# A spiking recommender on one core: filler transposes of the identity behind every transpose of the first stage

## The chip, the cores and the metric

The kernel runs on one core of one Trainium2 chip. The metric is the time of one execution on the device in microseconds (us), the median of three runs. Engines are named as in the profile: PE (matmuls and transposes; PEld its weight loads), DVE (vector), ACT (scalar), POOL (which issues the gathers) and SP (which issues plain DMAs).

## The reference, cut to what matters

The inputs are 1024 sequences of 50 item numbers, their lengths, and a table of 100001 rows of 128 floats. For every step t the row of the item is gathered and added to a running sum; the sum is divided by min(t, length), normalised over the batch, and fed into a leaky integrate-and-fire neuron. The mean of the spikes is multiplied by the whole table.

```python
e = emb[seq]                                  # 1024 x 50 x 128, row 0 counts as zero
prefix = jnp.cumsum(e, axis=1)
uF = prefix / denom[:, :, None]               # denom = min(t, length)
mean, var = uF.mean(axis=0), uF.var(axis=0)
y = (uF - mean) * lax.rsqrt(var + BN_EPS) * gamma + beta
def step(v, x):
    v = v + (x - v) / TAU
    spike = atan_spike(v - V_TH)              # 1 where v >= V_TH
    return v - spike * V_TH, spike
_, spikes = lax.scan(step, v0, x_seq)         # over the 50 steps
scores = spikes.mean(axis=0) @ emb.T          # 1024 x 100001
```

## The kernel before, in words

The program is written out in the order in which each engine works; there is no scheduler (`manual_schedule`), and each engine runs its own instructions in order.

**First stage** (lines 171 to 444): the 50 steps of the neuron, with the batch along the free dimension (1024 columns) and the 128 features on partitions. In step t:

- POOL has issued eight indirect DMAs (`gather`, line 204), each 128 rows of the table, into one of two tiles `e` (`gp`, line 177, two buffers). The gather of step t + 2 is issued after the transposes of step t and goes into the tile that they have read.
- PE transposes the eight blocks of 128x128 into `pre` (line 327), two PSUM banks `pre[0]` and `pre[1]`, adding to what is there: `pre` is the running sum. Four transposes make a half of the batch (`h`).
- DVE scales each half to `uF` (line 338) and takes statistics (339, 345).
- PE adds a correction for item 0 to each half for the next step (`correct`, lines 279 to 288, two matmuls of 512 columns). It must wait until DVE has read the half.
- ACT and DVE normalise and step the neuron: r, q, a (349 to 375), count (300), v (379, 382), d (293).

In steps 42 and 44 (`T - 8`, `T - 6`, lines 395 to 408) PE also prepares one piece of 1024 table rows: eight transposes into `pt` (line 136), which takes the PSUM buffer of an older v, followed by a copy on ACT (152) and a subtraction on DVE (153) that split the values in two parts, hi and lo. The first piece also has a small memset on DVE (133).

`warm` (line 305) is a tile of two PSUM banks that the second stage uses first as `po_0_0` (418). `keep_busy(tile, times)` (307 to 309) transposes a tile into it over and over; nobody reads the result. Before the change it is called in the last step behind three transposes, four times each (`KQ // 2`, with `KQ` = 8), and once after the loop, 16 times (414).

**Second stage** (446 to the end): for each block of columns of the output, and each of the eight blocks of 128 batch rows, PE multiplies the counts by hi and lo (line 160), ACT and DVE take turns in scaling the result out of PSUM (511, 513), and SP stores it (169). 409.6 MB are written.

Of the kernel before, what the change touches and what calls it, by code (L numbers as in the profile page):

```python
# [20 lines left out]
P = 128  # L21
# [3 lines left out]
KQ = HALF // P  # L25
BANK = 512
# [13 lines left out]
def rec_kernel(  # L40
# [34 lines left out]
    ident = const.tile([P, P], F32, tag="ident", name="ident")  # L75
# [96 lines left out]
    with ExitStack() as ph:  # L172
# [134 lines left out]
        def keep_busy(tile, times):  # L307
            for k in range(times):
                nc.tensor.transpose(warm[:, k % KQ * P : (k % KQ + 1) * P], tile, ident)
# [6 lines left out]
        for t in range(T):  # L316
            last = t == T - 1
# [7 lines left out]
            for h, cs in enumerate(halves):  # L325
                for k in range(0, BANK, P):
                    nc.tensor.matmul(  # L327
                        pre[h][:, k : k + P],
                        lhsT=e[:, h * BANK + k : h * BANK + k + P],
                        rhs=ident,  # L330
                        start=False,
                        stop=last,
                        is_transpose=True,
                        skip_group_check=True,
                    )
                    if last and h and k + P < BANK:
                        keep_busy(ident, KQ // 2)
                nc.vector.scalar_tensor_tensor(uF[:, cs], rlen[:, cs], 1.0 / (t + 1), pre[h], ALU.max, ALU.mult)  # L338
                nc.vector.bn_stats(bs[:, h, :], uF[:, cs])  # L339
# [123 lines left out]
    for c, W in enumerate(WIDTHS):  # L463
# [34 lines left out]
        for n in range(NB):  # L498
# [26 lines left out]
            if n in (1, 4) and c >= MIDDLE and to_fetch < parts:  # L525
                g, k = divmod(to_fetch - SHIFT, GROUP)
# [26 lines left out]
```

## Time and profile before

| what | before |
|---|---|
| median of 3 runs | 1643.39 us (1637.56 to 1649.35) |
| the profiled execution's own time | 1576.4 us |
| its span, first to last instruction | 1574.6 us |
| PE busy | 1128.4 us, 72% of the span |
| DVE busy | 949.3 us, 60% |
| ACT busy | 673.4 us, 43% |
| POOL busy | 380.9 us, 24% |
| bytes written to HBM | 409.60 MB |

The page's second part cuts the span into 40 slices of 39.4 us; each digit is the share of the slice in which the engine was busy, in tenths. Its fifth part groups instructions: line, engine, operation, what is written and read, count, then busy time in us and the mean of one in ns, then how long the engine stood idle just before them and what ended that. In a timeline a line is: start in us, duration in us, engine, line, operation, count (xN for N merged ones), and in brackets the idle time before it and what ended it. A busy time of a group of overlapping matmuls is less than count times mean. The page's clock digits are those of recorded clock events; where none had been recorded yet, they show full clock.

### The profile page before, as it was taken

The page shows a single profiled execution, that of the slowest core. Times are in us where ns is not written, and L with a number is a line of the kernel's source. Part 1 is how long each engine was busy: PE and PEld are TensorE (multiplying, and loading weights), DVE is VectorE, ACT ScalarE, POOL GpSimd, SP SyncE. Part 2 cuts the span into 40 slices and gives each one's busy share as a digit, 9 for nine tenths or more (in the row PEclk, how much of TensorE's full clock was granted, in tenths as well). Part 3 has the DMA queues.
Part 4 walks back from the last instruction along what each step waited for, and adds up shares of the span by engine and source line. Part 5 has one row for each costly group of instructions (what it writes and reads, how often), then busy time and mean ns, then how long its engine had stood idle before and what let it go on. Part 6 is the DMA issues. An engine that isn't in the chain of part 4 may idle for free.

```text
span 1574.6 us, 12255 instructions
## 1 busy us (share of the span) xinstructions
PE 1128.4 (72%) x4464; PEld 799.5 (51%) x4464; DVE 949.3 (60%) x1127; ACT 673.4 (43%) x697; POOL 380.9 (24%) x406
## 2 busy tenths in 40 slices
PE   4544444444445998899888878888878878888884
PEld 2211111111122766677766666666666666666663
DVE  5777777777777655666555555555555545555552
ACT  2333333333333545555444444444444444444442
POOL 7777777777776000000000000000000000000000
PEclk9999999999975999999999999898999999999998
DMA  9711111111121899999999999999999999999998
GB/s 347 264 52 54 52 54 52 53 53 54 52 79 47 337 414 414 423 413 402 428 427 429 427 426 421 421 409 429 421 428 424 402 428 429 414 423 417 426 405 354
DMA packets 51313, 488.12 MB, mean 310 GB/s; under 512 B 10079, under 2 KB 10336, under 8 KB 30004
## 3 DMA queue, kind: packets, MB, share of 16 engines
q1 hardware_dynamic: 30752, 430.86, 65.1%
q0 software_dynamic: 12800, 26.24, 5.7%
q10 hardware_dynamic: 7700, 30.23, 4.7%
q8 instruction: 35, 0.57, 0.1%
q14 instruction: 26, 0.21, 0.0%
HBM read 77.69 MB, written 409.60 MB: 309 GB/s over the span
## 4 chain that ended last, share of the span: by engine, by line
DMA 48%; POOL 18%; PE 15%; issue 8%; DVE 5%; ACT 4%; ACTq 0%; SPq 0%; POOLq 0%; DVEq 0%
DMA scores<-o 42%; POOL e L207 18%; PE po L160 14%; DMA e<-in_L_rec_emb_table,idx 6%; DVE o L511 3%; ACT o L513 3%; DVE pairs L153 1%; ACT pairs L152 0%; PE pt L136 0%; ACT hi L152 0%; DVE lo L153 0%; PE pre L327 0%; DMA idx<-in_r_seq 0%; DVE bs L339 0%; DVE uF L338 0%
## 5 line engine op out<-in xcount | busy, mean ns | idle before, releaser
L511 DVE TENSOR_SCALAR o<-po 128x1024 f32<-128x1024 f32 (+1 forms) x391 | 467.3, 1214 | 329.5 <-DMA scores<-o 187.4
L513 ACT ACTIVATE o<-po 128x1024 f32<-128x1024 f32 x391 | 392.0, 1025 | 506.0 <-DMA scores<-o 362.7
L207 POOL DMA_INDIRECT e<-in_L_rec_emb_table,idx x400 | 380.2, 951 | 123.9 <-issue 112.5
L327 PE MATMUL pre<-ident,e 128*128 128x128 f32 x400 | 179.9, 463 | 227.3 <-DMA e<-in_L_rec_emb_table,idx 227.0
L160 PE MATMUL po<-pairs,countB 128*128 128x512 f32 (+1 forms) x1120 | 292.8, 408 | 57.8 <-ACT o L513 57.8
L160 PE MATMUL po<-pairs,countC 128*128 128x512 f32 (+1 forms) x840 | 240.1, 433 | 59.4 <-ACT o L513 53.4
L160 PEld LDWEIGHTS po<-pairs,countB 128*128 128x128 f32 x1120 | 211.8, 194 | 119.2 <-ACT o L513 76.7
L327 PEld LDWEIGHTS pre<-ident,e 128*128 128x128 f32 x400 | 73.4, 184 | 337.1 <-DMA e<-in_L_rec_emb_table,idx 336.4
L160 PEld LDWEIGHTS po<-pairs,countC 128*128 128x128 f32 x840 | 168.1, 208 | 112.1 <-ACT o L513 65.5
L153 DVE TENSOR_TENSOR pairs<-pt,pairs 128x1024 fp32r<-128x1024 f32 x70 | 85.2, 1218 | 94.9 <-ACT pairs L152 94.8
L338 DVE SCALAR_TENSOR_TENSOR uF<-rlen,pre 128x512 f32<-128x512 f32 x100 | 68.3, 683 | 109.6 <-PE pre L327 109.6
L136 PE MATMUL pt<-ident,rows 128*128 128x128 f32 (+1 forms) x768 | 104.4, 281 | 9.9 <-issue 4.9
L349 ACT ACTIVATE r<-mv,eps 128x1 f32<-128x1 f32 x50 | 14.7, 295 | 223.4 <-DVE mv L345 223.4
L136 PEld LDWEIGHTS pt<-ident,rows 128*128 128x128 f32 (+1 forms) x768 | 94.1, 147 | 27.1 <-issue 10.9
L160 PE MATMUL po<-hi,countB 128*128 128x512 f32 x208 | 85.6, 411 | 15.1 <-ACT o L513 13.5
L281 PE MATMUL pre<-zT,ls 128*128 128x512 f32 x100 | 77.5, 777 | 23.2 <-DVE uF L338 19.3
L152 ACT CAST pairs<-pt 128x1024 fp32r<-128x1024 f32 x70 | 70.1, 1014 | 41.2 <-PE pt L136 41.2
L160 PE MATMUL po<-lo,countB 128*128 128x512 f32 x208 | 83.4, 401 | 0.0
L293 ACT ACTIVATE d<-v,less 128x1024 bf16<-128x1024 f32 x49 | 54.6, 1114 | 64.8 <-DVE v L382 62.3
L160 PE MATMUL po<-hi,countC 128*128 128x512 f32 x156 | 66.7, 427 | 14.1 <-ACT o L513 12.6
L379 ACT ACTIVATE v<-uF,hgb,a 128x1024 f32<-128x1024 f32 x49 | 59.2, 1208 | 30.6 <-DVE a L375 30.5
L339 DVE BATCH_NORM_STATS2 bs<-uF 128x6 f32<-128x512 f32 x100 | 69.4, 694 | 3.5
(87 smaller groups left out, 851.8 us busy)
## 6 DMA issues: line engine op xcount, KB each, us to landing
scores<-o SPq DMA_DIRECT2D x96, 3072.0 KB, 19.8
scores<-o SPq DMA_DIRECT2D x32, 1536.0 KB, 8.9
scores<-o SPq DMA_DIRECT2D x30, 1024.0 KB, 7.9
rows<-in_L_rec_emb_table ACTq DMA_DIRECT2D x19, 1536.0 KB, 29.3
scores<-o SPq DMA_DIRECT2D x8, 2896.5 KB, 17.2
rows<-in_L_rec_emb_table SPq DMA_DIRECT2D x5, 3072.0 KB, 34.9
e<-in_L_rec_emb_table,idx POOLq DMA_INDIRECT x400, 2.5
rows<-in_L_rec_emb_table SPq DMA_DIRECT2D x2, 1024.0 KB
```

The costliest lines, as they stand in the source:

```text
L136: nc.tensor.transpose(pt[:, k0 : k0 + pw], r[:pw, k0 : k0 + D], ident[:pw, :pw])
L152: nc.scalar.copy(vh, vp)
L153: nc.vector.tensor_tensor(vl, vp, vh.bitcast(F32), ALU.subtract)
L160: nc.tensor.matmul(po[:, :kw], lhsT=counts[n], rhs=part[:, k0 : k0 + kw], start=j == 0, stop=j == 1,)
L207: nc.gpsimd.indirect_dma_start(out=es[t][:, n * P : (n + 1) * P], out_offset=None, in_=table, in_offset=bass.IndirectOffsetOnAxis(ap=idx[: ...
L281: nc.tensor.matmul(pre[h], lhsT=l, rhs=zT[:, h * BANK : (h + 1) * BANK], start=t == 0, stop=False, skip_group_check=True,)
L327: nc.tensor.matmul(pre[h][:, k : k + P], lhsT=e[:, h * BANK + k : h * BANK + k + P], rhs=ident, start=False, stop=last, is_transpose=True, ...
L338: nc.vector.scalar_tensor_tensor(uF[:, cs], rlen[:, cs], 1.0 / (t + 1), pre[h], ALU.max, ALU.mult)
L339: nc.vector.bn_stats(bs[:, h, :], uF[:, cs])
L379: nc.scalar.activation(vt, uF[:, cs], AF.Identity, bias=hgb[:, 1:2], scale=a)
L511: nc.vector.tensor_scalar_mul(o[:, h0 : h0 + hw], po[:, :hw], 1.0 / T)
L513: nc.scalar.mul(o[:, h0 : h0 + hw], po[:, :hw], 1.0 / T)
```

## The change

Behind each of the eight transposes of line 327, in every step but the last, PE now transposes the identity nine times (`KQ + 1`) into `warm`. In the last step the fillers stay as they were.

```diff
@@ -333,7 +333,9 @@
                         is_transpose=True,
                         skip_group_check=True,
                     )
-                    if last and h and k + P < BANK:
+                    if not last:
+                        keep_busy(ident, KQ + 1)
+                    elif h and k + P < BANK:
                         keep_busy(ident, KQ // 2)
                 nc.vector.scalar_tensor_tensor(uF[:, cs], rlen[:, cs], 1.0 / (t + 1), pre[h], ALU.max, ALU.mult)
                 nc.vector.bn_stats(bs[:, h, :], uF[:, cs])
```

## The prediction

> **What bounds the kernel now.** I read the page's parts 1, 2 and 5 first, then the timeline of one step (around 265 us), of the end of the first stage (500 to 522 us) and of the two steps that also prepare table rows (434 to 474 us), and last the table of windows for the granted clock.
>
> ```profile
> span 1574.6 us, 12255 instructions
> ...
> PE   4544444444445998899888878888878878888884
> ...
> POOL 7777777777776000000000000000000000000000
> ...
> L207 POOL DMA_INDIRECT e<-in_L_rec_emb_table,idx x400 | 380.2, 951 | 123.9 <-issue 112.5
> L327 PE MATMUL pre<-ident,e 128*128 128x128 f32 x400 | 179.9, 463 | 227.3 <-DMA e<-in_L_rec_emb_table,idx 227.0
> ```
>
> The first stage is the 12.9 slices in which POOL works, 0 to about 511 us. PE is less than half busy there and waits for gathers. POOL never waits for anything but its own 0.30 us issue: a gather each 0.95 + 0.30 = 1.25 us. The timeline shows the beat:
>
> ```profile
> 264.20 0.94 POOL L207 DMA_INDIRECT e<-in_L_rec_emb_table,idx  x1 [0.30 <-issue]
> 265.45 0.95 POOL L207 DMA_INDIRECT e<-in_L_rec_emb_table,idx  x1 [0.30 <-issue]
> 265.48 0.18 PEld L327 LDWEIGHTS pre<-ident,e 128*128 128x128 f32 x1 [1.07 <-DMA e<-in_L_rec_emb_table,idx]
> 266.67 0.18 PEld L327 LDWEIGHTS pre<-ident,e 128*128 128x128 f32 x1 [1.01 <-DMA e<-in_L_rec_emb_table,idx]
> 267.19 0.69 DVE L338 SCALAR_TENSOR_TENSOR uF<-rlen,pre 128x512 f32<-128x512 f32 x1 [2.47 <-PE pre L327]
> 267.93 0.79 PE L281 MATMUL pre<-zT,ls 128*128 128x512 f32 x1 [0.35 <-DVE uF L338]
> ```
>
> Eight gathers make a step of 10.0 us. The transpose is 1.0 us of waiting and little work. So the stage is POOL's 400 x 1.25 = 500 us; nothing that makes PE faster there can shorten it, and PE matters only if its own step passes 10.0 us or if it falls so far behind that something waits.
>
> What a filler costs, and at which clock, stands at the stage's end and in the second stage:
>
> ```profile
> 504.49 0.48 PE L327 MATMUL pre<-ident,e 128*128 128x128 f32 x1
> 504.75 1.06 PE L309 MATMUL warm<-ident 128*128 128x128 f32 x4
> 507.28 2.61 PE L309 MATMUL warm<-ident,near 128*128 128x128 f32 x16
> ...
> 741.32 1.03 PE L136 MATMUL pt<-ident,rows 128*128 128x128 f32 x8
> ```
>
> Four cold fillers: (1.06 - 0.421 of one) / 3 = 0.213 us apart. Eight warm transposes of the same shape: (1.03 - 0.271) / 7 = 0.109 us apart. In the 16, durations fall from 421 to 273 ns and the window 508 to 509 us has a clock of 0.65 between 0.50 and 1.00. The stage before is cold, whatever its row of clock digits says: the same transposes take 470 ns and more at 265 us.
>
> [...] a burst of nothing but 16 transposes at 443.5 to 447.2 us left the next matmul at 0.50 us where that line takes 0.77 to 0.80, and the fillers of 503.6 to 508.7 us, with PE idle some 0.15 us in each 1.25, lifted the clock as well. [...]
>
> **The change part by part.** It adds 49 x 8 x 9 = 3528 pairs of weight load and transpose, no wait, no DMA, and removes nothing.
>
> 1. *Steady steps.* Warm PE work: 8 x 10 x 0.109 = 8.72 us, plus the two corrections of line 281 at about 0.226 us each (pitch of the warm 128x512 matmuls of line 160: 12 in 2.88 us, one 0.39): 0.45. Sum 9.17 us, under 10.0. It hides behind the gathers, with 0.83 us to spare per step. Per gather PE is busy some 1.1 of 1.25 us, as busy as the fillers that lifted the clock, so it should stay warm. DVE's uF needs only the transposes before the last nine, and the correction's wait for uF (1.26 us now) is filled by those nine. Cost 0. Without the warm clock the step would be 80 x 0.213 + 2 x 0.43 = 17.9 us.
>
> 2. *First step.* Its eight gathers have landed by 16.4 us and PE is cold. Fillers run cold to about 20.6 us [...]: 20 of the 80. The other 60 take 6.6 us: done 27.2, the last real one at 26.2 to 26.5. Step 2's gather overwrites the same e buffer (two buffers, lines 177 and 205) and was issued at 25.15. POOL loses 1.4 us, for good. [...]
>
> 3. *Steps 42 and 44* (lines 395 to 408). Here PE, in order, waits for DVE before it can prepare table rows, while gathers pile up:
>
> ```profile
> 443.30 0.17 DVE L133 MEMSET rows<- 1x128 f32 x1
> 443.56 1.94 PE L136 MATMUL pt<-ident,rows 128*128 128x128 f32 x8 [4.87 <-issue]
> 445.30 1.91 PE L327 MATMUL pre<-ident,e 128*128 128x128 f32 x8
> 448.46 0.50 PE L281 MATMUL pre<-zT,ls 128*128 128x512 f32 x1 [1.25 <-DVE uF L338]
> ...
> 462.02 1.94 PE L136 MATMUL pt<-ident,rows 128*128 128x128 f32 x8 [3.31 <-DVE count L300]
> ```
>
> Before, the backlog of eight went through in 1.9 us. Now it carries 72 fillers, and the 5 us of idling have made PE cold. Walking it through: preparing ends 445.1; cold to 447.3, one group of ten; seven groups x 1.09 = 7.6, to 454.9 (last real transpose 453.9, before 446.8); corrections to 455.4. Step 44: 8.7 us, to 464.1, last real 463.1 against 456.7: 6.4 us late. Its count on DVE ends 4.8 us after uF starts, so PE waits again to 468.3, prepares cold to 470.0, and is cold to about 473: step 45's last real one at 479.2. Each later step takes 8.7 + 0.5 = 9.2 us: 488.4 (step 46), 497.6 (47), 506.8 (48), where before has 497.0. The lag of 9.8 us shrinks by only 0.8 a step and has four steps. Step 46 ending at 488.4 also holds the gather of step 48 (485.8 before) 2.9 us; that lies inside the lag.
>
> 4. *End.* From step 48's last transpose on, DVE and ACT run a chain without slack (497.55 to 511.1 us: uF, statistics, count twice, negv, near, the last uF). It moves by 9.8 less 0.2 for warm latency = 9.6 us. The last step's fillers are unchanged and 20 transposes take 2.2 us, hidden behind that chain.
>
> 5. *Second stage.* Unchanged work, already at full clock at 511 us. Stores start at 513 us and share DMA with nothing before, and later blocks wait on them, so a late start passes through. Gain from a warm PE at its opening: nothing left to gain.
>
> Sum: 1.4 + 9.6 = 11.0 us. On the profiled execution 1576.4 + 11.0 = 1587.4; its span is 1574.6. The median of the runs, 1643.39, lies 67 us above the profiled one, and nothing in the profile says where; I add the difference to the median: 1654.4. Bounds of it: no re-cooling at both waits makes the lag 5.5 us[...]: +5 to +15.
>
> **Rivals.**
> - *A, hidden.* The two waits of DVE shrink or the lag is absorbed: 0 to +5, so 1643 to 1649. For it: DVE is busy only 7.2 us a step (71.9 of 100 us in the table of windows). Against: PE gains back only 0.8 us a step.
> - *B, uF waits for the ninth filler* if the semaphore comes behind them. Then the correction ends 1.2 us after the fillers, the step is 8.7 + 1.2 = 9.9 us, and no lag is ever made up: the first step's 7.5 us add to the later ones, about +20 to +25: 1666. Against: each instruction here is followed by its own waiter.
> - *C, PE does not stay warm.* It decides once the mean pitch passes (10.0 - 0.5) / 80 = 0.119 us. All cold: (17.9 - 10.0) x 48 = +380, 2020 us. Half the time: +170, 1815. [...] against: both bursts above.
> - *D, faster.* The unexplained 67 us are a cold PE in the second stage of unprofiled runs, which a warm arrival mends. A cold stretch costs half its length, so it outweighs the 11 us once there are over 22 us of it; all 67 mended would give 1587. Against: in the trace 16 fillers suffice to open at full clock.
>
> **How the numbers follow.** Forecast 56 in 100, A 22, B 10, C 8, D 4. About 1%, 16.4 us, is what a measurement tells from no change. Slower by more: all of C, most of B, and a seventh of the forecast (its upper bound with the runs' spread of 6 us): 24. Faster: D, 4. Within: 72. Range: from A's end less the spread, 1637, to B's end with it, 1675; it leaves out C, D and some of the edges. The forecast's own range is 1648 to 1660.
>
> **What would show it.** Right: line 327 at 273 ns instead of 463 through the stage, POOL still 1.25 us a gather, step period 10.0 us, fillers 0.109 us apart; gathers of step 48 late by some 3 us; last uF about 11 us later; the second stage unchanged in length. Wrong: POOL waiting on PE in most steps (C or B), fillers 0.213 us apart in mid-stage (C), a second stage of another length (D).

## The result and the profile after

The changed kernel takes 1710.0 us (median; 1707.46 to 1710.99) against 1641.63 us (1637.56 to 1649.35) of the kernel before: ratio 1.0411 [1.0387, 1.0434], slower by 68 us where 11 were forecast. One thing is needed to read any number below: in some sessions every execution of the kernel before takes about 1575 us (called a 1575 session here) and in others the median is 1638 to 1645 (a 1640 session), and the profile shown with the kernel before (1574.6 us) is of the first kind, while the medians that the forecast started from, the comparison above and the profile after are of the second.

The page of the changed kernel, with the rows that answer to those of before and the fillers' rows:

```profile
span 1709.0 us, 19311 instructions
...
PE   6888888888887878889898888888887888887884
...
POOL 6656666565666440000000000000000000000000
PEclk9899989989999898999999999899999889999998
...
L309 PE MATMUL warm<-ident 128*128 128x128 f32 x3540 | 490.4, 285 | 79.5 <-issue 77.9
L309 PEld LDWEIGHTS warm<-ident 128*128 128x128 f32 x3540 | 427.4, 147 | 113.5 <-issue 109.3
...
L207 POOL DMA_INDIRECT e<-in_L_rec_emb_table,idx x400 | 381.3, 953 | 247.7 <-PE pre L327 138.1
...
L340 DVE SCALAR_TENSOR_TENSOR uF<-rlen,pre 128x512 f32<-128x512 f32 x100 | 68.7, 687 | 240.1 <-remote 131.8
...
L327 PE MATMUL pre<-ident,e 128*128 128x128 f32 x400 | 113.1, 284 | 6.9 <-issue 4.4
```

PE is warm, as forecast: line 327 at 284 ns instead of 463, fillers at 285. Three waits are new. POOL, which hardly waited, has 138.1 us of waiting for the last transpose of a step. DVE's uF waits 131.8 us for something that the profile cannot name ("remote": a semaphore update is recorded there, but no instruction that could have made it ended shortly before). And PE stands idle in front of its own fillers for 77.9 us ("issue": a wait for nothing that the profile shows). One step in the timeline (start, duration, then what ran; the idle time before it in brackets):

```profile
247.98 0.27 PE L327 MATMUL pre<-ident,e 128*128 128x128 f32 x1
248.44 0.14 PEld L309 LDWEIGHTS warm<-ident 128*128 128x128 f32 x1 [0.42 <-issue]
249.83 1.52 PE L309 MATMUL warm<-ident 128*128 128x128 f32 x9 [1.58 <-issue]
...
249.86 0.69 DVE L340 SCALAR_TENSOR_TENSOR uF<-rlen,pre 128x512 f32<-128x512 f32 x1 [4.80 <-remote]
...
251.14 0.42 PE L327 MATMUL pre<-ident,e 128*128 128x128 f32 x1
...
251.83 0.94 POOL L207 DMA_INDIRECT e<-in_L_rec_emb_table,idx  x1 [3.00 <-PE pre L327]
...
257.58 0.27 PE L327 MATMUL pre<-ident,e 128*128 128x128 f32 x1
...
261.86 0.69 DVE L340 SCALAR_TENSOR_TENSOR uF<-rlen,pre 128x512 f32<-128x512 f32 x1 [3.40 <-remote]
```

The transpose at 257.58 is the fourth of its step and ends at 257.85. The uF that needs it starts at 261.86, four microseconds later, with DVE idle for 3.40 of them. While that update is under way PE first runs on and then stops among its fillers, as at 248.4 to 249.8; the eighth transpose of the earlier step comes late (251.14), and POOL, which needs it for the next gather, waits 3.00 us. The two uF waits marked "remote" lie 12.0 us apart: that is the step here, not 10.0. Taken from the starts of the first uF of steps 1 and 40, the step is 12.5 us on average.

Where the time lies is read from the issue of the first store of scores, the end of the first stage:

| kernel and session | first store at | from there to the end of the span |
|---|---|---|
| before, 1575 session (the profile shown earlier) | 513.3 us | 1061.3 us |
| before, 1640 session (g1_before below) | 572.0 us | 1061.1 us |
| after, 1640 session (the profile above) | 649.7 us | 1059.3 us |
| after, 1575 session (h1_after below) | 522.9 us | 1058.6 us |

These are the lines of the stores, in the order of the table (shortest, median and longest issue in ns, then the start of the first and of the last):

```profile
L169 SPq DMA_DIRECT2D scores<-o x172: 332/332/528, 513.3 to 1556.7; - x172
...
L169 SPq DMA_DIRECT2D scores<-o x172: 332/332/420, 572.0 to 1615.2; - x172
...
L169 SPq DMA_DIRECT2D scores<-o x172: 332/332/360, 649.7 to 1691.1; - x172
...
L169 SPq DMA_DIRECT2D scores<-o x172: 332/332/367, 522.9 to 1563.6; - x172
```

Nearly all of every difference, that between the two kinds of session included, is in the first stage.

### The profile page after: what moved, and what is told of

It is laid out like the page before. It is cut to its first block, busy times and chain, and to the rows that moved or that the text cites. A ratio compares the mean times of both kernels' runs of the same rounds, so it can differ in the third digit from the quotient of the medians.

```text
span 1709.0 us, 19311 instructions
## 1 busy us (share of the span) xinstructions
PE 1421.0 (83%) x7992; PEld 1190.2 (70%) x7992; DVE 954.4 (56%) x1127; ACT 673.4 (39%) x697; POOL 382.0 (22%) x406
## 4 chain that ended last, share of the span: by engine, by line
PE 41%; DMA 40%; issue 7%; DVE 5%; ACT 4%; POOL 1%; ACTq 0%; POOLq 0%; SPq 0%; DVEq 0%
DMA scores<-o 39%; PE warm L309 24%; PE po L160 13%; DVE o L513 3%; PE pre L327 3%; ACT o L515 2%; PE pre L281 1%; POOL e L207 1%; DVE pairs L153 1%; PE pt L136 1%; ACT pairs L152 0%; DMA e<-in_L_rec_emb_table,idx 0%; ACT hi L152 0%; DVE lo L153 0%; DVE bs L341 0%
## 5 line engine op out<-in xcount | busy, mean ns | idle before, releaser
L309 PE MATMUL warm<-ident 128*128 128x128 f32 x3540 | 490.4, 285 | 79.5 <-issue 77.9
L309 PEld LDWEIGHTS warm<-ident 128*128 128x128 f32 x3540 | 427.4, 147 | 113.5 <-issue 109.3
L207 POOL DMA_INDIRECT e<-in_L_rec_emb_table,idx x400 | 381.3, 953 | 247.7 <-PE pre L327 138.1
L340 DVE SCALAR_TENSOR_TENSOR uF<-rlen,pre 128x512 f32<-128x512 f32 x100 | 68.7, 687 | 240.1 <-remote 131.8
L327 PE MATMUL pre<-ident,e 128*128 128x128 f32 x400 | 113.1, 284 | 6.9 <-issue 4.4
L160 PE MATMUL po<-pairs,countA 128*128 128x512 f32 x280 | 69.7, 398 | 3.9 <-ACT o L515 3.3
```

What stands on the lines that cost most here:

```text
L160: nc.tensor.matmul(po[:, :kw], lhsT=counts[n], rhs=part[:, k0 : k0 + kw], start=j == 0, stop=j == 1,)
L207: nc.gpsimd.indirect_dma_start(out=es[t][:, n * P : (n + 1) * P], out_offset=None, in_=table, in_offset=bass.IndirectOffsetOnAxis(ap=idx[: ...
L327: nc.tensor.matmul(pre[h][:, k : k + P], lhsT=e[:, h * BANK + k : h * BANK + k + P], rhs=ident, start=False, stop=last, is_transpose=True, ...
```

## The experiments

All are timed against the kernel before in their own session. The expectations name theories by letters; what each letter says stands in them or beside them. My first theory, R, was that PE alone is the cause, a limit on the instructions that it completes, which no run shows; the first batch tried it with other fillers. The rate of the second stage that e2_few's expectation names is read from the profile of the kernel before: 142 matmuls and 141 weight loads between 730 and 760 us, 9.4 per us.

**Session 1, the kernel before at 1575.42 us.** Unchanged kernel; four fillers instead of nine; four matmuls of 512 columns instead of nine transposes; nine transposes of 32 rows.

```diff
 e2_few
-                        keep_busy(ident, KQ + 1)
+                        keep_busy(ident, KQ // 2)
 e3_wide    (wide: matmul(warm half, lhsT=zT[:, :P], rhs=zT[:, :BANK]))
-                        keep_busy(ident, KQ + 1)
+                        wide(4)
 e4_narrow  (narrow: transpose(warm[:, .. 32], ident[:32, :], ident[:32, :32]))
-                        keep_busy(ident, KQ + 1)
+                        narrow(KQ + 1)
```

> The kernel before, unchanged, for a second profile. Its one profile has a span of 1574.6 us while its runs took 1637 to 1649; the changed kernel has no such gap (profile 1709.0, runs 1707 to 1711). If the gap is a matter of how one execution is recorded, this profile shows about 1575 again; if the profile on record is a rare fast execution, it shows about 1640, and says in which stage the 65 us lie.

> Four fillers behind each transpose instead of nine: 80 instructions on PE per step where the change has 164 (a weight load and a matmul each). Theory R [...]: 8 per us are under the rate that the second stage sustains, no stalls, step 10.0 us, the time of before within 5 us. Theory B (PE being busy slows the stage through the clock or shared memories): about half of the 68 us, 1665 to 1685. My prediction's view (only lags at the end matter): within 5 us of before.

> Four matmuls of 512 columns (0.227 us each when warm) instead of nine transposes: PE as busy as in the change (4 x 0.227 + 0.11 = 1.02 of 1.25 us), half the instructions. Output unchanged. Theory R: no stalls in the middle of a step, step 10.0 us, time that of before or up to 12 us more (lag after the waits of steps 42 and 44). Theory B: as slow as the change, 1700 to 1715.

> Nine fillers of 32 columns and 32 rows instead of 128: as many instructions as the change, but less array work [...]. Theory R: the same stalls, step 12 us or more, 1700 us or more. Theory B: much of the loss gone, under 1670.

Measured: e1_before 1573.72 us, so the early profile repeats. e2_few 1572.87, ratio 0.9986 [0.9979, 0.9992]. e3_wide 1580.74, 1.0036 [1.0024, 1.0049]. e4_narrow 1736.98, 1.1022 [1.1004, 1.1041]. None of them has a wait of uF for "remote", so e2_few and e3_wide, though both lie where my theory had them, can't test it: there were no late updates to explain. e4_narrow is slow for another reason: the two rows of its page and its window from 200 to 300 us (columns: busy time and count for PE, PEld, DVE, ACT, POOL, then clock, DMA share, GB/s) are

```profile
L313 PE MATMUL warm<-ident 32*128 32x32 f32 x3528 | 456.3, 292 | 0.0
...
L331 PE MATMUL pre<-ident,e 128*128 128x128 f32 x400 | 185.5, 466 | 0.0
```

```profile
200.00:300.00 100.00, 100.00 (x639) 79.23 (x639) 55.03 (x91) 27.38 (x30) 58.13 (x62) 1.00 0.16 42
```

Line 331, the real transpose, takes 466 ns: PE is busy for 100.00 of the 100 us and is not warm, whatever the column of the clock says (1.00). The page's clock digits are no evidence where no clock event was recorded; durations are. So e4_narrow is rival C of the prediction with another filler and says nothing of the late updates. Its time lies in the range of theory R (1700 or more) by accident.

**Session 2, the kernel before at 1644.60 us.** The change itself; six; eight; and the wide ones in steps 0 to 41 only.

```diff
 f2_six
-                        keep_busy(ident, KQ + 1)
+                        keep_busy(ident, KQ - 2)
 f3_eight
+                        keep_busy(ident, KQ)
 f4_wide_early
-                    if not last:
-                        keep_busy(ident, KQ + 1)
-                    elif h and k + P < BANK:
+                    if t < T - 8:
+                        wide(4)
+                    elif last and h and k + P < BANK:
```

> The change itself, on the same chip as the kernel before and the two dose runs. The first comparison gave 1710.0 against 1641.6, but 26 later executions of the kernel before all took 1574 to 1577 us, and the profile of the change loses (12.7 - 10.0) x 49 = 132 us in the first stage. If those profiles are what the executions do, this is 1705 to 1712 against 1575, a ratio of 1.085; if the first comparison stands, 1.04.

> Six fillers behind each transpose: 116 instructions of PE a step, 11.6 per us at a step of 10.0. Theory R (a limit near 12.9 instructions per us when they come for long, as the change's 164 in 12.7 us): no stall, step 10.0, 1570 to 1580. Theory T (stalls come from any run of fillers at the warm pitch, whatever the mean rate): still stalls, some 1620.

> Eight fillers, one less than the change: 148 instructions a step. PE's own time would be 8 x 9 x 0.109 + 0.45 = 8.3 us, well under 10.0. Theory R: 148 / 12.9 = 11.5 us a step, 49 x 1.5 = 73 us more: 1630 to 1665. A theory in which only PE's own time counts: 1575 to 1585.

> The four wide matmuls instead of nine transposes, in steps 0 to 41 only, none from step 42 on. The wide fillers in all steps cost 5 us (1580.7 against 1575.4). If that is the lag after the waits of steps 42 and 44, as my prediction has it, it is gone: within 1.5 us of before. If it is a price of fillers in every step, 42 of 49 parts stay: about 1580.

Measured: f1_after 1710.72, ratio 1.0408 [1.0386, 1.0429]; f2_six 1674.94, 1.0186 [1.0167, 1.0205]; f3_eight 1683.71, 1.0242 [1.0221, 1.0263]; f4_wide_early 1658.8, 1.0091 [1.0062, 1.0121]. More fillers cost more. But f4_wide_early, with half the change's PE instructions and none of the fillers from step 42 on, still has 122.5 us of uF waiting for "remote", and it loses 14.2 us where 1.5 or 5 were expected. Six fillers, which theory R had at no cost, lose 30.3. And the kernel before is 69 us slower than in session 1. Something acts here without any filler.

**Session 3, the kernel before at 1637.86 us, another chip.** The kernel before with its profile; the change; the four wide fillers; four transposes. The edits are those above (g3_wide is e3_wide, g4_few is e2_few).

> The kernel before, unchanged, on whatever chip comes. Theory K (chips differ: on some, semaphore updates of PE come microseconds late in the first stage, with or without the change): if this chip's time is near 1642 us, the profile shows a first stage about 67 us longer than 511 us, with DVE's uF or POOL's gathers waiting behind recorded ends of transposes, and a second stage of about 1064 us. If the chip's time is near 1575, the profile repeats the one on record. Rival (the late updates come only with the fillers): a chip at 1642 shows a first stage of about 511 us and loses its 67 us in the second stage.

> The change itself. Theory K: on a chip where the kernel before takes 1575, steps of 10.0 us and +5 to +15 us (my sum of 11 was made for such a chip); on one where it takes 1642, +68 us again. Rival (the stalls come from the number of fillers, whatever the chip): stalls behind the seventh transpose and a step of 12.7 us on any chip, about 1705 us.

> Four matmuls of 512 columns in place of nine transposes, in all steps but the last: PE as busy (97%), with half as many instructions. On a chip at 1575: +5 to +6, as before. On a chip at 1642, theory K with the number of instructions as what matters: about +10 to +15, far less than the change's 68. Rival (PE's busy time is what matters): +60 or more there.

> Four transposes of the identity instead of nine, in all steps but the last. On a chip at 1575: -2 to 0, as before. On a chip at 1642, if the number of instructions sets the loss: about +10 to +25, less than six fillers (+30). If the loss there starts only with a threshold: 0.

Measured: g1_before 1634.95; g2_after 1686.51, ratio 1.0293 [1.0268, 1.0318]; g3_wide 1669.06, 1.0188 [1.0164, 1.0212]; g4_few 1659.07, 1.0118 [1.009, 1.0145]. The page of g1_before and a piece of its timeline:

```profile
span 1633.1 us, 12255 instructions
...
L207 POOL DMA_INDIRECT e<-in_L_rec_emb_table,idx x400 | 380.3, 951 | 181.1 <-issue 112.5
...
L338 DVE SCALAR_TENSOR_TENSOR uF<-rlen,pre 128x512 f32<-128x512 f32 x100 | 68.1, 681 | 155.9 <-remote 113.9
```

```profile
165.07 0.47 PE L327 MATMUL pre<-ident,e 128*128 128x128 f32 x1 [0.80 <-DMA e<-in_L_rec_emb_table,idx]
...
170.01 0.47 PE L327 MATMUL pre<-ident,e 128*128 128x128 f32 x1 [0.66 <-DMA e<-in_L_rec_emb_table,idx]
...
172.95 0.69 DVE L338 SCALAR_TENSOR_TENSOR uF<-rlen,pre 128x512 f32<-128x512 f32 x1 [5.44 <-remote]
...
182.75 0.69 DVE L338 SCALAR_TENSOR_TENSOR uF<-rlen,pre 128x512 f32<-128x512 f32 x1 [8.38 <-remote]
182.99 0.94 POOL L207 DMA_INDIRECT e<-in_L_rec_emb_table,idx  x1 [4.57 <-remote]
183.49 0.80 PE L281 MATMUL pre<-zT,ls 128*128 128x512 f32 x1 [9.00 <-DVE uF L338]
```

The fourth and eighth transposes of this step end at 165.54 and 170.48. The two uF that need them start at 172.95 and 182.75, so the signal is 7.4 and 12.3 us on its way, in a kernel without a filler. The trace's records of semaphore updates agree: an update of PE's semaphore stands at 172.93 and one at 182.73 us, each 0.02 us before the start. 19 waits for "remote", 113.9 us in all and up to 10.7 each, stretch the first stage to 572.0 us, 58.7 more than in the profile shown earlier, and the whole execution is longer by as much (1633.1 against 1574.6 us). So the difference that the forecast could not place lies in the first stage. The other direction is prompt: the second uF ends at 183.44 and PE's correction starts at 183.49; its 9.00 us of waiting are uF's lateness passed on.

g3_wide and g4_few have about the same number of PE instructions and quite different work. Their windows from 200 to 300 us:

```profile
200.00:300.00 100.00, 87.20 (x362) 63.39 (x362) 62.67 (x107) 31.84 (x35) 65.74 (x70) 0.90 0.17 45
```

```profile
200.00:300.00 100.00, 65.50 (x371) 56.25 (x372) 63.61 (x109) 32.93 (x36) 66.72 (x71) 0.76 0.18 47
```

PE is busy 87.20 us in the first (g3_wide) and 65.50 in the second (g4_few), but POOL, the beat of the stage, gets through nearly the same: 70 and 71 gathers, where the kernel before gets through 81 in the same window of the profile shown earlier. The first store comes at 607.2 and 598.2 us; of those 9.0 us, 7.4 are also there in session 1 (519.7 and 512.3), where they are the lag that PE's length makes. If that lag may be carried over from one kind of session to the other, which no run shows, the two lose the same, and the number of PE's instructions sets the rest. The forecasts of g3_wide missed on both sides, though: +31 us, where +10 to +15 was the theory of the number and +60 or more the rival of busy time. And length is not without weight when a step is nearly full: from eight to nine fillers in session 2 the instructions of a step grow from 148 to 164, and the loss from 39 to 66 us.

**Session 4, the kernel before at 1575.24 us, on the same chip as session 2.** The change once more; all 72 fillers of a step behind its eighth transpose; the change in steps 0 to 41 only.

```diff
 h2_behind
-                        keep_busy(ident, KQ + 1)
+                        keep_busy(ident, (KQ + 1) * KQ * (h and k + P == BANK))
 h3_early
-                    if not last:
+                    if t < T - 8:
                         keep_busy(ident, KQ + 1)
-                    elif h and k + P < BANK:
+                    elif last and h and k + P < BANK:
```

> The change itself once more, to learn what it costs on the chip that comes. If the kernel before takes about 1575 us there (no late semaphore updates of PE): my sum of +11 us (bounds +5 to +15), steps of 10.0 us. Rival (the fillers alone bring the stalls, on every chip): +50 to +130. If the kernel before takes about 1640: +49 to +69, as on the two chips of that kind so far.

> The same 72 fillers per step, all behind the eighth transpose, so that no filler stands between the eight real ones. Where the kernel before takes about 1640: theory M (what counts is how many instructions PE completes, its updates come behind them): +45 to +70, as with the change. Rival N (an update is late because fillers stand close behind the transpose that makes it): under +25. Where the kernel before takes about 1575: +5 to +15, as the change.

> The change in steps 0 to 41 only, none from step 42 on. Where the kernel before takes about 1575: the lag of 9.6 us goes, 0 to +2 is left. Where it takes about 1640: the change's loss less seven forty-ninths of it for the steps without fillers: +40 to +60.

Measured: h1_after 1583.66, ratio 1.0059 [1.0043, 1.0076], which is +8.4 us; h2_behind 1574.0, 0.9992 [0.9984, 1.0001]; h3_early 1575.83, 1.0003 [0.9995, 1.0012]. That refutes my idea of two kinds of chip: one chip showed both kinds of session. And it shows what the change costs when updates are prompt. The page and the timeline of h1_after:

```profile
span 1581.5 us, 19311 instructions
...
POOL 7777777777776000000000000000000000000000
...
L309 PE MATMUL warm<-ident 128*128 128x128 f32 x3540 | 438.0, 273 | 0.0
L207 POOL DMA_INDIRECT e<-in_L_rec_emb_table,idx x400 | 380.4, 951 | 127.7 <-issue 116.7
...
L327 PE MATMUL pre<-ident,e 128*128 128x128 f32 x400 | 112.5, 283 | 16.8 <-DMA e<-in_L_rec_emb_table,idx 16.6
```

```profile
25.47 0.94 POOL L207 DMA_INDIRECT e<-in_L_rec_emb_table,idx  x1 [0.68 <-PE pre L327]
...
454.86 0.27 PE L327 MATMUL pre<-ident,e 128*128 128x128 f32 x1
...
464.06 0.27 PE L327 MATMUL pre<-ident,e 128*128 128x128 f32 x1
...
479.21 0.27 PE L327 MATMUL pre<-ident,e 128*128 128x128 f32 x1
479.75 0.94 POOL L207 DMA_INDIRECT e<-in_L_rec_emb_table,idx  x1 [3.85 <-PE pre L327]
...
506.81 0.27 PE L327 MATMUL pre<-ident,e 128*128 128x128 f32 x1
...
517.55 0.67 DVE L340 SCALAR_TENSOR_TENSOR uF<-rlen,pre 128x512 f32<-128x512 f32 x1
```

POOL keeps its beat, the fillers never wait, and the last transposes of steps 43, 44, 45 and 48 stand where the prediction had them (453.9, 463.1, 479.2, 506.8 as the end of step 48). Taking the fillers out of steps 42 to 48 (h3_early) takes the whole loss away. So does placing all of a step's fillers behind its eighth transpose (h2_behind), where I had expected +5 to +15: the last transpose of step 48 then ends at 497.1 us, as in e1_before, and at 507.1 in h1_after.

**Session 5, the kernel before at 1644.83 us.** No filler; SP loads eight small pieces more per step. Theory R is now that the landings of DMAs and PE's instructions together make the updates late, rival P that PE's instructions alone do.

```diff
 i3_extra, behind gather(t + 2)
+                for n in range(KQ):
+                    nc.sync.dma_start(out=scrap[:, n, :], in_=table[n * P : (n + 1) * P, :8])
```

> No filler at all: the kernel before with eight more small loads by SP in every step (128 pieces of 32 bytes each into a tile that nobody reads), so that about twice as many DMA landings are signalled in the first stage while PE does no more than before. Where the kernel before takes about 1640: theory R [...]: +20 to +100 with stalls like those before. Rival P [...]: within 5. Where the kernel before takes about 1575: within 5 by either, a control.

Measured: 1648.75 us, ratio 1.0023 [1.0013, 1.0033], or +3.9. That is within the rival's bound and far from theory R's 20 to 100. As many plain loads as there are gathers, with their landings, cost hardly anything.

**Session 6, the kernel before at 1637.60 us.** The change with the gathers of steps 10 to 49 left out, so that those steps transpose old rows and the scores are other ones; and h2_behind again.

```diff
 i1_dry, in gather(t)
+            if t >= T // 5:
+                es[t] = kept[t % 2]
+                return
-            es[t] = gp.tile([P, B], F32, tag="e", name=f"e_{t}")
+            kept[t % 2] = es[t] = gp.tile([P, B], F32, tag="e", name=f"e_{t}")
```

> The change with all fillers, but the gathers of steps 10 to 49 left out: those steps transpose the rows of steps 8 and 9 again, so the counts are other ones. POOL then sets no beat: PE's own step is 9.2 us, and some forty steps of it end about 32 us earlier than at 10.0. Where the kernel before takes about 1640: theory P (PE's instructions alone overload something there): the step from 10 on stays at 12 us or more, with PE stopping for nothing shown. Rival G (it needs the gathers at the same time): 9.2 us a step, no stops. Where the kernel before takes about 1575: 9.2 us by either, about 1545 to 1555 us.

> All 72 fillers of a step behind its eighth transpose, once more. It took 1574 us where the kernel before took 1575. Where the kernel before takes about 1640: theory M (the number of PE's instructions counts): +45 to +70. Rival N (a filler close behind a transpose makes that transpose's update late): under +25.

Measured: i1_dry 1581.64, ratio 0.9662 [0.9645, 0.968]; i2_behind 1683.97, 1.0279 [1.0262, 1.0296], which is +46, theory M: placed out of the way the fillers cost nearly what they cost in g2_after (+49). i1_dry within one execution:

```profile
20.00:120.00 100.00, 86.82 (x706) 81.05 (x705) 57.08 (x97) 29.27 (x32) 63.41 (x67) 0.97 0.54 194
200.00:300.00 100.00, 100.00 (x893) 98.53 (x892) 77.82 (x131) 39.56 (x44) 0.00 (x0) 1.00 0.00 1
```

```profile
258.40 0.27 PE L331 MATMUL pre<-ident,e 128*128 128x128 f32 x1
...
260.89 0.69 DVE L344 SCALAR_TENSOR_TENSOR uF<-rlen,pre 128x512 f32<-128x512 f32 x1 [1.74 <-PE pre L331]
...
267.60 0.27 PE L331 MATMUL pre<-ident,e 128*128 128x128 f32 x1
...
270.10 0.69 DVE L344 SCALAR_TENSOR_TENSOR uF<-rlen,pre 128x512 f32<-128x512 f32 x1 [1.01 <-PE pre L331]
```

As long as POOL gathers (67 in the first window) PE gets through 706 matmuls in 100 us. Once the gathers are over it does 893, and the same transpose of the next step comes exactly 9.20 us later (258.40, 267.60), as the prediction's 9.17 had it. The steps with gathers take 8.9 to 14.6 us each. Gathers alone do not hold PE up: in session 4, with 80 of them in the first window, h1_after gets through 891 matmuls there. So theory P is refuted too: in a 1640 session it takes PE's instructions and the gathers at the same time. That is rival G. Leaving out the gathers takes away POOL's instructions, their landings and PE's waits for them together; which of these counts is not shown.

## Why the prediction was wrong, and where it was right

*What bounds the kernel.* Right for the profile that it read, wrong for the executions that it was compared with. Its sentence "The median of the runs lies 67 us above the profiled one, and nothing in the profile says where; I add the difference to the median" treated the 67 us as a constant. In g1_before the difference lies in the first stage (572.0 instead of 513.3 us), in the very waits between PE, DVE and POOL that the change loads.

*Step 1, steady steps, "Cost 0".* This is the step that failed. Its parts held: the pitch of 0.109 us, the warm clock, 9.17 us of PE work (9.20 measured where nothing disturbs it), and cost 0 in session 4. What it took for granted was that a step lasts 10.0 us, set by POOL alone, and that a finished transpose is known at once to DVE and POOL. In the 1640 sessions PE's signals come late (7.4 and 12.3 us in g1_before): from step 1 to step 40 a step takes 11.4 us on average before the change (g1_before), 12.0 with it in the same session (g2_after) and 12.5 in the profile above. The first store moves from 572.0 us to 625.9 and 649.7. That is the cost that step 1 put at 0; with the lag of steps 3 and 4 the change comes to +49 us in session 3, +66 in session 2 and +68 in the first comparison.

*Step 2, first step: 1.4 us.* In session 4 the gather starts at 25.47 instead of 25.15, 0.3 us. That the fillers run cold up to 20.6 us was an estimate of mine, and so is what it gives, 1.4 us. In the profile after, PE is warm sooner: the first three transposes of that step start at 16.43, 18.56 and 19.85 us and take 0.41, 0.42 and 0.27 us.

*Steps 3 and 4, the lag: 9.6 us.* Right in mechanism and size. That PE is cold again behind a wait shows in h1_after: the real transpose takes 0.27 us at 464.06, and 0.42 us at 470.94, behind 3.43 us of idling and the eight transposes of table rows; the nine fillers behind it take 1.66 us, the next nine 1.15. The lines of h1_after agree with the walk to a microsecond, and the last uF moves from 507.97 to 517.55 (9.6 us), the first store from 513.3 to 522.9 (9.6 us). The wait of POOL came one step sooner than I had it, at the gathers of step 47 behind step 45, and is 3.85 us instead of 2.9. e3_wide shows a lag of the same kind with another filler (its last uF comes 5.9 us after that of e1_before), and h3_early keeps 1.5 us of it.

*Step 5, second stage.* It passes a late start through. It takes 1058.6 us in h1_after, and 1061.3 and 1059.0 in two executions of the kernel before (the profile shown earlier, e1_before), so no gain is shown there. The sum of 11.0 comes out as +8.4 [+6.8, +12.0 by the ratio's interval] in session 4; 1.1 us of the difference is step 2. The upper bound of +15 was an estimate of mine, for longer cold stretches.

*The rivals.* A (0 to +5) did not happen: in h1_after nothing absorbed the lag. B had uF wait for the ninth filler; what is seen are waits of up to 4.9 us, in 46 of 100 uF, and h1_after has none of them. C did not happen: with nothing but transposes and the two corrections, PE is warm (line 327 at 284 ns in the profile after, 283 in h1_after); its case shows in e4_narrow, with narrow fillers (line 331 at 466 ns). D is refuted: the 67 us are not in the second stage. "POOL waiting on PE in most steps" was rightly named as the mark of a failed step, but the mechanism behind it was on no list.

*What stays open.* What PE's signals and the gathers share in a 1640 session is not shown. It is not the number of PE's signals that grows: between 100 and 500 us the trace of the kernel before (1575 session) holds 398 updates of PE's semaphore and that of h1_after 181, since hardly a filler makes one. One hint is in the page's list of DMA issues. In a 1575 session it has the time to landing of a gather (h1_after), in a 1640 session it can't give one (g1_before):

```profile
e<-in_L_rec_emb_table,idx POOLq DMA_INDIRECT x400, 2.5
```

```profile
e<-in_L_rec_emb_table,idx POOLq DMA_INDIRECT x400
```

The trace of g1_before holds 7239 semaphore updates, that of the same kernel in a 1575 session 13223. They are missing where the gathers run: between 200 and 300 us there are 318 against 1542, between 700 and 1500 us 3435 against 3320. In i1_dry, once the gathers are over, they are nearly whole again (201 between 200 and 300 us; h1_after has 208 there beside the landings of its gathers). So records are missing in the very stretches in which updates are late, but no run shows that the two have one cause: every execution timed here was also recorded, and none without a record was tried. The 3.9 us of i3_extra speak against the landings alone. What puts a session into one kind or the other is open too.

## What to carry to other kernels

Ask first whether the profile in hand is of the executions that will be compared: when its span lies 4% below the medians, the difference belongs to some stage, and a forecast of "hidden" work in that stage is not covered until it is known which. Where a stage lives on short signals from PE to other engines while gathers run, count PE's instructions as well as its busy time: 72 fillers per step cost 8 us in one session (and nothing there when placed behind the eighth transpose) and 46 to 68 us in others. Fillers around a forced wait also push the work behind them (+8.4 us in h1_after, +0.6 in h3_early without those of steps 42 to 48): leave them out of the steps before a stage's end, where no slack is left to win the lag back.

## What the runs showed of the hardware

- From the end of a transpose to the start of the uF that waited for it were 7.4 and 12.3 us in g1_before, a 1640 session, and 0.04 us in i1_dry once the gathers were over (the eighth transpose of a step ends at 270.06 us, its uF starts at 270.10). The time from the first store to the end lies between 1058.6 and 1061.8 us in every run, in both kinds of session.
- One and the same chip ran the same kernel at 1575.24 us in one session and at 1644.60 in another.
- Transposes of 32 rows kept PE busy for 100.00 of 100 us (e4_narrow) and left it cold: 466 ns for the real transpose, where it is 463 before the change and 283 among transposes of 128 rows (h1_after).
- Matmuls of 512 columns with half as many instructions kept PE as warm as nine transposes (the real transpose takes 286 ns in g3_wide, 280 in g2_after) and cost a third less in the same 1640 session (+31 against +49 us).
- Fillers that PE wrote to other PSUM banks did not slow DVE's reads by more than 1%: a uF takes 687 ns in the profile after, 681 in g1_before and 683 in the profile of the kernel before.
